# A depthwise convolution whose images share their padding and whose kernel rows sit in a deeper ring

## The chip, the cores and the metric

The kernel runs on one core of a Trainium2 chip. The metric is the device time of one execution in microseconds (us); the time given is the median of several executions. A separate, profiled execution gives the records that the tables show.

## The reference

The program is four layers on a batch of 8 images of 384 channels and 32 x 32 points. Layers 0 and 1 are state-space blocks, the second with an MLP. The change touches only what follows them:

```
# layer 2: depthwise 13x13, plus six smaller and dilated depthwise kernels, each with its own scale and shift
out = bn(dwconv(x, w_lk, 1)) + sum(bn(dwconv(x, w, r)) for w, r in branches)
# layer 3: a pointwise product, then depthwise 13x13 and a per-channel factor, then gelu
x_pw = bn(einsum('bchw,oc->bohw', x, pw_w)) + x
out = gelu(bn(dwconv(x_pw, dwk_w)) + bn(x_pw * dw1_w))
```

All is in float32. The kernel folds the seven branches of layer 2 into one 13 x 13 kernel per channel, and the per-channel factor of layer 3 into the centre of its kernel.

## The kernel before

Three stages follow the state-space layers: a depthwise convolution (tensor x3 to x4), the pointwise product (x4 to x5), and a second depthwise convolution (x5 to the output). The last MLP of the layers writes x3 in three thirds of 128 channels (`mlp_out`, L714, and `mlp_store`, L721); its two products are the matmuls of L695 (first) and L708 (second). That part has an order written out by hand. The three stages after it are issued in the order that the framework finds from the program's order and its waits.

x3 and x5 hold, for each channel, image row and image, 32 points between two gaps of six zeros, so WIDE = 44 columns. The eight images of one row lie behind each other: 352 numbers.

A depthwise convolution (`Depthwise.run`) handles four channels at a time, a group; 96 groups make the 384 channels. Its work per group:

- Two image transfers on GpSimd's queue (L958) put the 32 rows of four channels into a tile `xp`, two channels on partitions 0 to 31 and two on 64 to 95, the second shifted by two numbers.
- Four kernel transfers (L962), one for each shift of one column, put windows of the kernel table into a tile `wt`, 64 KB each. Two go over SyncE's queue, one over ScalarE's and one over GpSimd's.
- Four copies on VectorE (L975 twice, L976, L977) fill the other partitions of `xp` with the same rows shifted by one or two numbers. They cover two channels of n - 1 or n - 2 numbers, n = 8 x WIDE.
- Sixteen matmuls on TensorE (L982): for each of four column offsets (4j) and four channels, 128 partitions by 32 columns of weights against 8 images x 32 points.
- One activation on ScalarE (L987) adds the bias and takes the result out of PSUM, and a store on ScalarE's queue (L988) writes it.

`xp` and `wt` are rings of eight tiles. Before group 0, six groups are loaded; in group g the transfers of group g + 6 are issued (AHEAD = 6). A tile is free for its next transfer when the matmuls of the group eight earlier, group g - 2, have read it. All 16 tiles are cleared on GpSimd when the object is made (L949), and the three output tiles of the pointwise stage after them (L1005). The memory of these tiles partly lies over tiles of the layers before; a first write waits until those have been used.

The pointwise stage (`Pointwise.run`) takes 16 blocks of 512 points: a load on SyncE's queue (L1011), nine matmuls for each of them (L1016), activation, an addition on VectorE (L1021) into a tile with gaps, and one store on ScalarE's queue.

A queue's issues run in the order in which they stand in its engine's program. The built program also gives every transfer one of eight semaphores, eight for those of SyncE and ScalarE together and eight for GpSimd's, in turn; an issue waits for the earlier transfer on its semaphore.

Of the kernel before, what the change touches and what calls it, by code (L numbers as in the profile page):

```python
# [9 lines left out]
F32 = mybir.dt.float32  # L10
# [6 lines left out]
P = 128  # L17
B = 8
# [9 lines left out]
HW = 32  # L28
# [4 lines left out]
HK = 64  # L33
KP = 4
PAD = KS // 2
WIDE = HW + 2 * PAD
NG = C // 4
EPS = 1e-5
PAST = 16100
# [27 lines left out]
class Plan:  # L67
# [3 lines left out]
    def __init__(self):  # L71
        self.slots = {}
# [151 lines left out]
def layers(tc, k, a, vec, x0, x1, x2, x3, lasting, got):  # L224
# [16 lines left out]
    with ExitStack() as st:  # L241
# [39 lines left out]
        nc.vector.memset(carry[:, KD], 0.0)  # L281
        rows_out = wp.tile([P, T // HW, WIDE], F32, name="rows_out")
        nc.gpsimd.memset(rows_out, 0.0)
# [648 lines left out]
class Depthwise:  # L932
# [4 lines left out]


    NB, AHEAD = 8, 6

    def __init__(self, tc, st):
        nc = self.nc = tc.nc
        self.keep = st.enter_context(tc.tile_pool(name="d_keep", bufs=1, reuse_waits="tile"))
        self.work = st.enter_context(tc.tile_pool(name="d_work", bufs=4, reuse_waits="tile"))
        self.psum = st.enter_context(tc.tile_pool(name="d_ps", bufs=4, space=PSUM, reuse_waits="tile"))
        self.wts = [self.keep.tile([P, 4, HW, KP], F32, name=f"wt{i}") for i in range(self.NB)]
        self.xps = [self.keep.tile([P, 4, B * WIDE], F32, name=f"xp{i}") for i in range(self.NB)]
        for t in self.wts + self.xps:
            nc.gpsimd.memset(t, 0.0)  # L949

    def load(self, g, src, table):
        nc, n = self.nc, B * WIDE
        wt, xp = self.wts[g % self.NB], self.xps[g % self.NB]
        for h in range(2):
            rows = bass.AP(
                src.tensor, src.offset + (g * P + 2 * HW * h) * n + 2 * h, [[n, HW], [HW * n, 2], [1, n - 2 * h]]
            )
            nc.gpsimd.dma_start(xp[2 * HW * h : 2 * HW * h + HW, 2 * h : 2 * h + 2, 0 : n - 2 * h], rows)  # L958
        for s, queue in enumerate((nc.sync, nc.scalar, nc.sync, nc.gpsimd)):
            at = table.offset + (16 * g + s) * HK * KP  # L960
            windows = bass.AP(table.tensor, at, [[KP, HW], [4 * HK * KP, 4], [1, HW * KP]])
            queue.dma_start(wt[HW * s : HW * (s + 1)].rearrange("p q r j -> p q (r j)"), windows)  # L962

    def run(self, src, table, bias, func, store):
        nc = self.nc
        n = B * WIDE
        for g in range(self.AHEAD):
            self.load(g, src, table)
        for g in range(NG):
            wt, xp = self.wts[g % self.NB], self.xps[g % self.NB]  # L970
            if g + self.AHEAD < NG:
                self.load(g + self.AHEAD, src, table)
            for h in range(2):
                low, q = 2 * HW * h, slice(2 * h, 2 * h + 2)
                nc.vector.tensor_copy(xp[low + HW : low + 2 * HW, q, 0 : n - 1], xp[low : low + HW, q, 1:n])  # L975
            nc.vector.tensor_copy(xp[2 * HW :, 0:2, 0 : n - 2], xp[: 2 * HW, 0:2, 2:n])  # L976
            nc.vector.tensor_copy(xp[: 2 * HW, 2:4, 2:n], xp[2 * HW :, 2:4, 0 : n - 2])  # L977
            ps = self.psum.tile([P, T], F32, tag="ps", name="ps")
            x = xp.rearrange("p q (b c) -> p q b c", c=WIDE)
            for j in range(KP):  # L980
                for q in range(4):
                    nc.tensor.matmul(  # L982
                        ps[HW * q : HW * (q + 1), : B * HW], wt[:, q, :, j], x[:, q, :, 4 * j : 4 * j + HW],
                        start=j == 0, stop=j == KP - 1,
                    )
            o = self.work.tile([P, B, HW], F32, tag="o", name="o")
            nc.scalar.activation(o, ps[:, : B * HW], func, bias=bias[:, g : g + 1])  # L987
            nc.scalar.dma_start(store(g), o)  # L988
# [42 lines left out]
@with_exitstack  # L1031
def network(ctx: ExitStack, tc: tile.TileContext, a: dict, out: bass.AP):
    nc = tc.nc
    const = ctx.enter_context(tc.tile_pool(name="const", bufs=1))
    dram = ctx.enter_context(tc.tile_pool(name="dram", bufs=1, space=DRAM))

    k = {}
    k["avg"] = const.tile([P, P], F32, name="avg")
    nc.vector.memset(k["avg"], 1.0 / C)
    k["eps"] = const.tile([P, 1], F32, name="eps")  # L1040
    nc.vector.memset(k["eps"], EPS)
    k["one"] = const.tile([P, 1], F32, name="one")
    nc.vector.memset(k["one"], 1.0)
    k["minus"] = const.tile([P, 1], F32, name="minus")
    nc.vector.memset(k["minus"], -1.0)
    k["fold"] = const.tile([P, 32], F32, name="fold")
    k["gate"] = const.tile([P, KC * B], F32, name="gate")
    k["gate_b"] = const.tile([P, KC * B], F32, name="gate_b")
    vecs = const.tile([P, NVEC], F32, name="vecs")
    nc.sync.dma_start(vecs, a["vecs"])  # L1050

    def vec(name):
        at, width = VEC[name]
        return vecs[:, at : at + width]

    x_in = a["x"].rearrange("b c h w -> b c (h w)")
    x0 = [x_in[b] for b in range(B)]
    x1 = [dram.tile([C, L], F32, name=f"x1_{b}") for b in range(B)]
    x2 = [dram.tile([C, L], F32, name=f"x2_{b}") for b in range(B)]
    x3 = dram.tile([C, HW, B, WIDE], F32, name="x3")  # L1060
    x4 = dram.tile([C, HW * B * HW], F32, name="x4")
    x5 = dram.tile([C, HW * B * WIDE], F32, name="x5")

    k["one_at_R"] = vec("one_at_R")
    got = {"b2": const.tile([P, NG], F32, name="b2"), "b3": const.tile([P, NG], F32, name="b3")}
    got["pw"] = const.tile([P, 2 * KC], F32, name="pw_norm")
    layers(tc, k, a, vec, x0, x1, x2, x3, dram, got)

    with ExitStack() as st:

        past = st.enter_context(tc.tile_pool(name="past", bufs=1, reuse_waits="tile"))
        past.tile([P, PAST], F32, name="past")
        past_ps = st.enter_context(tc.tile_pool(name="past_ps", bufs=1, space=PSUM, reuse_waits="tile"))
        past_ps.tile([P, 4 * T], F32, name="past_ps")
        conv = Depthwise(tc, st)
        point = Pointwise(tc, st, conv.psum, a["pw"])
        x4_rows = x4.rearrange("c (r n) -> (c r) n", r=HW)
        conv.run(
            x3, got["k2"], got["b2"], AF.Identity,
            lambda g: x4_rows[g * P : (g + 1) * P].rearrange("p (b w) -> p b w", w=HW),  # L1080
        )
        point.run(x4, x5, got["pw"][:, 0:KC], got["pw"][:, KC:])
        out_rows = out.rearrange("b c h w -> (c h) b w")
        conv.run(x5, got["k3"], got["b3"], AF.Gelu, lambda g: out_rows[g * P : (g + 1) * P])
# [113 lines left out]
```

## Time and profile before

| | us |
|---|---|
| median of 3 executions | 6946.22 |
| range | 6943.45 to 6947.82 |
| the profiled execution's own time | 6954.78 |
| its span | 6952.9 |
| first copy of the first convolution | 6373.28 |
| first pointwise matmul | 6599.89 |
| first copy of the second convolution | 6734.08 |

| over the whole span | busy us | share |
|---|---|---|
| TensorE, matmuls | 5904.4 | 85% |
| TensorE, weight loads | 2097.6 | 30% |
| VectorE | 5851.6 | 84% |
| ScalarE | 4475.0 | 64% |
| GpSimd | 5429.7 | 78% |

How to read what follows: PE is TensorE (PEld its weight loads), DVE VectorE, ACT ScalarE, POOL GpSimd, SP SyncE. L982 is line 982 of the kernel before. In a timeline, a row gives the start and the duration in us, the engine, the line, the operation, the tiles, how many instructions are merged, and in brackets the idle time before and what ended it. In a list of waits a row gives who waited for whom, the total in us, how often, and the longest. In a table of stretches a row gives the stretch, its length and each engine's busy time. The DMA share is the mean busy share of 16 DMA engines; transfers overlap in it, so it can exceed 1. Transfers issued by GpSimd are instructions with a duration of their own in its timeline, one per transfer.

The three last stages take 580 us of the span of 6952.9. The busy shares of the page are nearly all of the layers before them, so the stages are to be read by themselves.

### The profile page before, as it was taken

What the parts mean: (1) busy time and instruction counts of PE and PEld (TensorE: products, weight loads), DVE (VectorE), ACT (ScalarE), POOL (GpSimd) and SP (SyncE); (2) the same over time, 40 slices, a digit from 0 to 9 for tenths busy, and PEclk for the clock granted to TensorE, in tenths of its full rate; (3) what the DMA queues carried; (4) which work ended last, traced back from release to release, by engine and by line L of the source; (5) the groups of instructions that cost most, each with busy time, mean ns of one, the idle gap of its engine ahead of it and who ended that gap; (6) DMA issues with size and microseconds to landing.
All of it is one profiled execution on the core that took longest, in us unless ns stands there. A gap on an engine that the chain in (4) does not pass through costs nothing. (4 is left out here: it accounts for less than half of the span.)

```text
span 6952.9 us, 78464 instructions
## 1 busy us (share of the span) xinstructions
PE 5904.4 (85%) x22562; PEld 2097.6 (30%) x22562; DVE 5851.6 (84%) x4975; ACT 4475.0 (64%) x7478; POOL 5429.7 (78%) x3146
## 2 busy tenths in 40 slices
PE   6777788888888888888888888888889889877898
PEld 2222222222322232222222232223223223324645
DVE  2899998999889888888889988988888998863849
ACT  4776666767676767767676767676677667742222
POOL 2888888888788878888888878887877888754626
PEclk7888898999999999999999999999999889999999
DMA  4665555666666566666666665656666666645979
GB/s 123 166 176 155 154 160 149 167 168 173 171 165 181 157 169 167 161 168 167 167 165 172 167 174 161 176 155 174 165 157 168 160 171 172 161 108 131 264 224 242
DMA packets 960565, 1169.60 MB, mean 168 GB/s; under 512 B 314057, under 2 KB 552713, under 8 KB 960137
## 3 DMA queue, kind: packets, MB, share of 16 engines
q1 hardware_dynamic: 787848, 1062.39, 57.5%
q10 hardware_dynamic: 147712, 55.08, 3.1%
q0 software_dynamic: 24576, 47.12, 2.3%
q8 instruction: 184, 3.01, 0.2%
q14 instruction: 245, 2.00, 0.1%
HBM read 909.39 MB, written 204.21 MB: 160 GB/s over the span
## 5 line engine op out<-in xcount | busy, mean ns | idle before, releaser
L532 POOL TENSOR_TENSOR dbu<-B,ru 128x1024 f32<-128x1024 f32 x1536 | 3584.9, 2357 | 136.9 <-DMA B<-bc 56.8
L525 ACT ACTIVATE h<-rd,A 128x512 f32<-128x512 f32 x3072 | 2117.5, 691 | 861.8 <-DVE hc L561 524.8
L553 DVE TENSOR_TENSOR_SCAN h<-h,state,dbu 128x512 f32<-128x512 f32 x1152 | 1482.4, 1287 | 221.1 <-ACT h L525 79.6
L561 DVE TENSOR_TENSOR hc<-h,C 128x1024 f32<-128x1024 f32 x1152 | 1410.8, 1225 | 129.2 <-PE acc L583 14.5
L556 DVE TENSOR_TENSOR_SCAN h<-h,dbu 128x1024 f32<-128x1024 f32 x576 | 1318.1, 2288 | 239.0 <-ACT h L525 182.4
L572 POOL TENSOR_TENSOR hc<-dbu,C 128x1024 f32<-128x1024 f32 x384 | 903.5, 2353 | 736.7 <-DVE dbu L556 337.1
L583 PE MATMUL acc<-hc,fold 128*32 128x512 f32 x6144 | 1174.6, 663 | 340.7 <-DVE hc L561 257.9
L415 PE MATMUL mm<-xt,wi 128*128 128x512 f32 x2232 | 1123.3, 642 | 43.6 <-ACT delta L491 18.9
L695 PE MATMUL f<-mx,wi 128*128 128x512 f32 x1152 | 610.5, 638 | 139.9 <-ACT fh L699 111.0
L708 PE MATMUL f<-fh,wo 128*128 128x512 f32 x1152 | 587.0, 628 | 82.0 <-DMA wo<-in_fc_dram 66.8
L415 PEld LDWEIGHTS mm<-xt,wi 128*128 128x128 f32 x2232 | 424.7, 202 | 745.4 <-issue 447.8
L604 PE MATMUL mm<-u,wo 128*128 128x512 f32 x1152 | 579.4, 643 | 38.5 <-DMA wo<-in_l_out_dram 31.4
L583 PEld LDWEIGHTS acc<-hc,fold 128*32 128x32 f32 x6144 | 165.9, 112 | 1163.7 <-DVE hc L561 548.5
L553 DVE TENSOR_TENSOR_SCAN dbu<-h,state,dbu 128x512 f32<-128x512 f32 x384 | 470.4, 1267 | 14.0 <-ACT h L525 8.6
L556 DVE TENSOR_TENSOR_SCAN dbu<-h,dbu 128x1024 f32<-128x1024 f32 x192 | 437.9, 2281 | 39.8 <-ACT h L525 29.3
L439 PE MATMUL mm<-xp,taps 128*64 128x512 f32 x1536 | 407.0, 653 | 33.8 <-DMA xp<-xp 12.4
L982 PE MATMUL ps<-xp,wt 128*32 128x256 f32 x6144 | 376.1, 387 | 66.0 <-DVE xp L977 30.3
L958 POOL DMA_DIRECT2D xp<-x x384 | 215.4, 565 | 276.8 <-DMA x<-q_out 139.8
L305 ACT ACT_TABLE_LOAD x289 | 370.8, 1283 | 5.9 <-PEq L1186 0.7
L695 PEld LDWEIGHTS f<-mx,wi 128*128 128x128 f32 x1152 | 209.3, 196 | 499.4 <-issue 248.5
L580 PE MATMUL acc<-u,skip 128*128 128x512 f32 x384 | 226.8, 675 | 153.7 <-DVE u L588 153.5
L425 ACT ACTIVATE xp<-mm,b_in 64x512 f32<-64x512 f32 x384 | 261.5, 681 | 140.8 <-PE mm L415 138.3
(152 smaller groups left out, 5876.2 us busy)
## 6 DMA issues: line engine op xcount, KB each, us to landing
ru<-uu SPq DMA_DIRECT2D x1536, 128.0 KB
rd<-dd SPq DMA_DIRECT2D x1536, 128.0 KB
wi<-w_in SPq DMA_DIRECT2D x372, 192.0 KB
xp<-xp SPq DMA_DIRECT2D x384, 128.5 KB
dd<-delta SPq DMA_DIRECT2D x192, 256.0 KB
uu<-delta SPq DMA_DIRECT2D x192, 256.0 KB
wo<-in_l_out_dram SPq DMA_DIRECT2D x96, 384.0 KB
wi<-fc_w SPq DMA_DIRECT2D x192, 192.0 KB
```

What stands on the lines that cost most here:

```text
L415: nc.tensor.matmul(s.ps[m], w[:, c], s.xt[:, c], start=c == 0, stop=c == KC - 1)
L439: nc.tensor.matmul(s.ps[d][64 * h : 64 * h + 64], taps[:, h, j], xp[h][:, 2 * j : 2 * j + T], start=j == 0, stop=j == 1,)
L525: nc.scalar.activation(y[:, q], s.dr[d][1][h][:, q], AF.Exp, scale=s.layer.A[:, at : at + 1])
L532: nc.gpsimd.tensor_tensor(dbu, s.B[g].unsqueeze(1).to_broadcast([P, 2, T]), s.ur[d][1][h], ALU.mult)
L553: nc.vector.tensor_tensor_scan(to[:, q], y[:, q], dbu[:, q], first, ALU.mult, ALU.add)
L556: nc.vector.tensor_tensor_scan(flat_to, flat_y, flat_b, first, ALU.mult, ALU.add)
L561: nc.vector.tensor_tensor(hc, to, s.C[g].unsqueeze(1).to_broadcast([P, 2, T]), ALU.mult)
L572: nc.gpsimd.tensor_tensor(hc, y, s.C[g].unsqueeze(1).to_broadcast([P, 2, T]), ALU.mult)
L583: nc.tensor.matmul(s.acc[d][32 * r : 32 * r + 32], k["fold"], tiles[r // 2][:, r % 2], start=False, stop=n == PER - 2)
L604: nc.tensor.matmul(s.ps[m], w[:, d], s.us[d], start=d == 0, stop=d == KD - 1)
L695: nc.tensor.matmul(s.ps[m], s.w["in", m][:, c], s.xt[:, c], start=c == 0, stop=c == KC - 1)
L708: nc.tensor.matmul(s.down, s.w["out", 2 * m + f // KD][:, f % KD], s.hs[f], start=f == 0, stop=f == KF - 1)
```

## The change

It does three things.

- The gap between two images of a row is shared: six zeros instead of twelve, WIDE = 38. A row of eight images has 304 numbers. The last image needs a gap behind it, so an `xp` tile has 12 numbers more than a row's, which stay zero. The matmuls take their 8 x 32 points from a slice that begins at 4j. The stored tensors x3 and x5 and the tiles that are written to them are narrower in the same way.
- The kernel rows have a ring of 24 tiles of their own (`NK`), of 2 KB a partition each, that is no longer cleared first. In group g the kernel transfers of group g + 22 are issued (`EARLY`), over the same queues as before; the images stay 6 ahead in a ring of 8.
- The kernel transfers of the first 22 groups are issued by a new function `early`, all four of each group on GpSimd's queue: for the first convolution ahead of its image transfers, for the second after the first convolution and ahead of the pointwise stage.

```diff
-WIDE = HW + 2 * PAD
+WIDE = HW + PAD
...
     NB, AHEAD = 8, 6
+    NK, EARLY = 24, 22
...
-        self.wts = [self.keep.tile([P, 4, HW, KP], F32, name=f"wt{i}") for i in range(self.NB)]
-        self.xps = [self.keep.tile([P, 4, B * WIDE], F32, name=f"xp{i}") for i in range(self.NB)]
-        for t in self.wts + self.xps:
+        self.wts = [self.keep.tile([P, 4, HW, KP], F32, name=f"wt{i}") for i in range(self.NK)]
+        self.xps = [self.keep.tile([P, 4, B * WIDE + 2 * PAD], F32, name=f"xp{i}") for i in range(self.NB)]
+        for t in self.xps:
             nc.gpsimd.memset(t, 0.0)
 
-    def load(self, g, src, table):
+    def kernels(self, g, table, queues):
+        wt = self.wts[g % self.NK]
+        for s, queue in enumerate(queues):
+            at = table.offset + (16 * g + s) * HK * KP
+            windows = bass.AP(table.tensor, at, [[KP, HW], [4 * HK * KP, 4], [1, HW * KP]])
+            queue.dma_start(wt[HW * s : HW * (s + 1)].rearrange("p q r j -> p q (r j)"), windows)
+
+    def early(self, table):
+
+        for g in range(self.EARLY):
+            self.kernels(g, table, [self.nc.gpsimd] * 4)
+
+    def images(self, g, src):
         nc, n = self.nc, B * WIDE
-        wt, xp = self.wts[g % self.NB], self.xps[g % self.NB]
+        xp = self.xps[g % self.NB]
...
-        for s, queue in enumerate((nc.sync, nc.scalar, nc.sync, nc.gpsimd)):
-            at = table.offset + (16 * g + s) * HK * KP
-            windows = bass.AP(table.tensor, at, [[KP, HW], [4 * HK * KP, 4], [1, HW * KP]])
-            queue.dma_start(wt[HW * s : HW * (s + 1)].rearrange("p q r j -> p q (r j)"), windows)
...
         for g in range(self.AHEAD):
-            self.load(g, src, table)
+            self.images(g, src)
         for g in range(NG):
-            wt, xp = self.wts[g % self.NB], self.xps[g % self.NB]
+            wt, xp = self.wts[g % self.NK], self.xps[g % self.NB]
             if g + self.AHEAD < NG:
-                self.load(g + self.AHEAD, src, table)
+                self.images(g + self.AHEAD, src)
+            if g + self.EARLY < NG:
+                self.kernels(g + self.EARLY, table, (nc.sync, nc.scalar, nc.sync, nc.gpsimd))
...
-            x = xp.rearrange("p q (b c) -> p q b c", c=WIDE)
             for j in range(KP):
+                x = xp[:, :, 4 * j : 4 * j + n].rearrange("p q (b c) -> p q b c", c=WIDE)
                 for q in range(4):
                     nc.tensor.matmul(
-                        ps[HW * q : HW * (q + 1), : B * HW], wt[:, q, :, j], x[:, q, :, 4 * j : 4 * j + HW],
+                        ps[HW * q : HW * (q + 1), : B * HW], wt[:, q, :, j], x[:, q, :, 0:HW],
...
+        conv.early(got["k2"])
         conv.run(
             x3, got["k2"], got["b2"], AF.Identity,
...
+        conv.early(got["k3"])
         point.run(x4, x5, got["pw"][:, 0:KC], got["pw"][:, KC:])
```

## The prediction

> **What bounds the kernel now.** I read the busy time by stretch first, then the timelines of VectorE, GpSimd and TensorE at the borders of the stages, then the waits and the chain. Stretches: first convolution from 6373 us, pointwise from 6599, second convolution from 6734 (columns: length, then busy us and instructions of PE, PEld, DVE, ACT, POOL, then clock, DMA share, GB/s).
>
> ```profile
> 6373.00:6590.00 217.00, 184.51 (x3060) 144.31 (x3064) 200.43 (x385) 44.84 (x95) 159.52 (x280) 0.97 0.93 259
> 6599.00:6727.00 128.00, 125.53 (x288) 55.28 (x288) 33.24 (x48) 37.30 (x48) 0.00 (x0) 0.98 0.66 219
> 6734.00:6947.00 213.00, 188.59 (x3048) 111.22 (x3048) 200.34 (x384) 44.80 (x95) 152.48 (x276) 0.99 1.06 249
> ```
>
> VectorE (DVE) works 200 us in each convolution, 384 copies. Its timeline shows that this is all it can do:
>
> ```profile
> 6387.61 0.52 DVE L975 COPY xp<-xp 32x702 f32<-32x702 f32 x1
> 6388.17 0.52 DVE L977 COPY xp<-xp 64x700 f32<-64x700 f32 x1
> ...
> 6390.38 0.52 DVE L977 COPY xp<-xp 64x700 f32<-64x700 f32 x1
> 6394.02 0.52 DVE L975 COPY xp<-xp 32x702 f32<-32x702 f32 x1 [3.12 <-PE ps L982]
> ```
>
> A copy starts every 0.551 us (0.522 at work, 0.030 between), so a group of four takes 2.206 and 96 groups 211.8. From 6373.28 to 6589.09 (215.8 us) the only wait is the 3.12 above; from 6734.08 to 6946.91 (212.8 us) there is none. VectorE is the bound of both. The runners-up are close. TensorE needs 1.96 us for a lone group, some 1.8 back to back (96 records, three groups, in 5.51). The stores on ScalarE's queue:
>
> ```profile
> ACT o L987 <- DMA out_dram<-o: 92.3, 57, 2.6
> PEld ps L982 <- DVE xp L977: 66.0, 93, 0.9
> ```
> ```profile
> 6429.88 3.99 DMA x<-o
> ...
> 6433.95 4.42 DMA x<-o
> ...
> 6438.45 5.23 DMA x<-o
> ```
>
> As built, a DMA issue on the SP or ACT queue waits for the eighth before it; a group issues four there, so a store waits for the store two groups back. In the first convolution TensorE starts 12 us late for want of kernel rows and catches up from 6403 to 6523 with 1,862 matmul records in 120 us, 32 a group: 2.06 us, 2.05 allowing for the 0.6% of records that the table shows missing of 3072. The chain of that time is stores of about 4.1 us each, two groups apart. So the store loop can do some 2.05, at DMA share 0.97.
>
> What sets the start of the first convolution is seen in GpSimd's (POOL's) timeline and TensorE's:
>
> ```profile
> 6302.64 5.46 POOL L1005 MEMSET q_out<- 128x2112 f32 x3
> 6360.43 1.27 POOL L958 DMA_DIRECT2D xp<-x  x2 [52.34 <-issue]
> 6361.70 0.56 POOL L962 DMA_DIRECT2D wt<-k_rows  x1
> 6362.24 1.07 POOL L958 DMA_DIRECT2D xp<-x  x2
> ```
> ```profile
> 6335.45 2.84 PE L695 MATMUL f<-mx,wi 128*128 128x512 f32 x6 [0.78 <-ACT fh L699]
> ```
>
> POOL stands idle from 6308 to 6360 (until x3's first third is stored) and issues images 13 us before VectorE, busy with its last residual add until 6373.25, takes them. That is all the slack an insertion in POOL's queue has there.
>
> [...] the trace has 2.31 from the first issue at 6731.77 to the copy at 6734.08. [...] an issue takes 0.54 us while VectorE rests, 0.57 beside it.
>
> **The change, part by part.**
> Narrower rows (44 to 38 columns, 352 to 304 an image row). Copies shrink from 702 and 700 to 606 and 604 elements: [...] with the same 0.030 between, 2.006 us a group. Saved 0.200 x 96 = 19.2 us in each convolution. The matmuls keep their 256 columns; their rows start at 8-byte instead of 16-byte steps, which I cost at nothing (bounds: 0 and, if a group rose from 1.96 to 2.1, +9 per convolution). The pointwise output falls from 1056 to 912 KB: 0.4 us off the last store (4.00 us in the chain), which opens the second convolution. x3's stores are hidden behind matmuls.
>
> Kernel rows 22 ahead. In steady state the queues carry the same 256 KB of kernels a group, the four issues each still after TensorE's group g-2; only the last 22 groups have none. The images fall from 175 to 152 KB, so a group moves 536 instead of 559 KB (-4.2%).
>
> The early loads, first convolution. 22 groups x 4 = 88 issues, all on POOL, ahead of the images. When can they start? The memsets of the old eight kernel tiles (3.8 us) go. But the tiles now reach further into memory of the layers: as built, the memset of the third q_out waits for the matmuls of the last first-MLP slice, which end at 6335.45 + 2.84 = 6338.3. With its 1.6 us (1824 elements at the row's 1858 ns for 2112) the first early issue comes at 6339.9. 88 x 0.54 = 47.5 (48 to 50 at 0.55 to 0.57), so POOL is free for images at 6387.4 to 6390; I take 6388.2. Plus the 2.3 us of the second convolution's start: first copy at 6390.5 instead of 6373.28, 17.2 us late. In return the kernels are there, and the 3.1 us wait goes. First convolution: copies end at 6390.5 + 192.6 + 0.5 = 6583.6, against 6589.1: -5.5.
>
> The early loads, second convolution. 88 issues, queued on POOL after image group 95, each tile after its last matmul: from about 6569 to 6618, 64 KB every 0.55 us, 119 GB/s beside the pointwise (219). Its matmuls take all 125.5 us and had one wait for a load, the first of 8.8 us; the sum of 338 GB/s is below the 390 that the trace shows in bursts. POOL's next work, images at 6732, waits anyway. Six groups of kernel loads that stood before the first pointwise input on the SP queue shrink to two, so I put the delay of that input at +0.5 (bounds -0.5 and +2).
>
> Second convolution: -19.2 -0.4. Its stores have 128-byte packets and the share is 1.06; no stretch shows how fast its store loop can go, only 2.206. Scaled from 2.05 by DMA share and bytes, 2.05 x 1.06/0.97 x 0.958 = 2.15; with slack, 2.006, for TensorE never waits for ACT there. For the 74 groups with kernels I take 2.05, nearer to the lower: +3.3 (bounds 0 and +10.7). In the first, 2.05 x 0.958 = 1.96 is below VectorE's 2.006: nothing.
>
> Sum: -5.5 + 0.5 - 19.2 - 0.4 + 3.3 = -21.3 us. The profiled execution took 6954.78 (span 6952.9), the median is 6946.22, 8.6 less; the difference lies in no stage, so I take the saving whole: 6946.2 - 21.3 = 6925.
>
> **The rivals.**
> (1) The start isn't late, because early issues fit in POOL's idle 52 us: for it, the idle time is longer than 47.5; against it, 30 us of it lie before the memset is released. 6925 - 17.2 = 6908.
> (2) The store loop takes the bound over in part, 2.06 to 2.15 in both convolutions. For it: stores already hold ACT for 92 us of 213, about 1 us behind TensorE. Against: ACT never holds TensorE in the second one. Without the 3.3 the sum is -24.6; with 148 groups x 0.054 to 0.144 us more, 6930 to 6943, middle 6936.
> (3) It ends slower: the store loop doesn't quicken at all. Place: the store's wait for the store two groups back. At 2.206 for the 148 groups with kernels, -24.6 + 148 x 0.2 = +5: 6951. It decides from 2.17, where 148 x (p - 2.006) is 24.6; from 2.27 it is over 0.2%.
> (4) The change doesn't do what it says (copies as long as before): 6946.2 - 24.6 + 38.4 = 6960; [...]
>
> **How the numbers follow.** Forecast 0.64 (6916 to 6932), (1) 0.05, (2) 0.18, (3) 0.10, (4) 0.03. 0.2% is 13.9 us, about what a measurement can tell: faster below 6932.3. The forecast nearly whole, (1) and a little of (2): faster 0.72. The rest of (2) and most of (3): same 0.23. Slower 0.05. Range: leave out (1), the upper half of (3) and (4): 6912 to 6946.
>
> **What would show it.** Right: copies of 0.472 us, 0.502 apart; POOL's first early issue near 6340 and first image near 6388; first copy near 6390; copies end near 6584; no 3.1 us wait; second convolution some 194 to 197 us. Wrong: images issued near 6360; VectorE waiting for images while ACT waits for stores (rivals 2, 3); the first pointwise input over 2 us later after the last copy than 10.8.

## The result and the profile after

| | before | after |
|---|---|---|
| median | 6946.22 us | 6968.72 us |
| range of 7 executions each | 6941.35 to 6951.60 | 6962.32 to 6977.39 |
| ratio, 95% interval | | 1.0033 [1.0021, 1.0044] |
| profiled execution (span) | 6954.78 (6952.9) | 6964.66 (6962.7) |

The change made the kernel 0.33% slower, 22.5 us between the medians. The forecast was 21.3 us faster.

Here are the stretches of after (the same columns as before: length, busy us and instructions of PE, PEld, DVE, ACT, POOL, then clock, DMA share, GB/s), from the first copy of each convolution and from the first pointwise matmul:

```profile
6406.00:6608.00 202.00, 189.54 (x3068) 111.52 (x3070) 187.52 (x384) 45.03 (x95) 159.22 (x285) 0.98 0.86 237
6618.00:6746.00 128.00, 126.42 (x288) 55.58 (x288) 32.53 (x47) 37.20 (x48) 27.09 (x51) 0.98 0.71 230
6753.00:6957.00 204.00, 184.00 (x3042) 146.64 (x3046) 185.57 (x384) 44.55 (x94) 147.09 (x261) 0.98 1.02 228
```

VectorE is busy 187.5 and 185.6 us instead of 200. Its timeline shows a late first copy, and copies that are not all of one length:

```profile
6406.65 0.47 DVE L986 COPY xp<-xp 32x606 f32<-32x606 f32 x1 [29.86 <-DMA xp<-x]
6407.16 0.49 DVE L987 COPY xp<-xp 64x604 f32<-64x604 f32 x1
...
6411.88 0.52 DVE L986 COPY xp<-xp 32x606 f32<-32x606 f32 x1
...
6417.80 0.47 DVE L987 COPY xp<-xp 64x604 f32<-64x604 f32 x1
6418.30 0.47 DVE L986 COPY xp<-xp 32x606 f32<-32x606 f32 x1
```

In the first convolution the list of waits of after has TensorE waiting for VectorE, so the copies are the bound there, and ScalarE waiting less for stores than in before, whose line comes last:

```profile
PEld ps L993 <- DVE xp L988: 52.7, 92, 0.8
ACT o L998 <- DMA x<-o: 47.4, 31, 4.0
```
```profile
ACT o L987 <- DMA x<-o: 79.4, 53, 3.8
```

VectorE has nothing to copy for 29.86 us after its last residual addition. TensorE's and GpSimd's timelines of after say why:

```profile
6338.15 2.84 PE L695 MATMUL f<-mx,wi 128*128 128x512 f32 x6 [0.78 <-ACT fh L699]
```

```profile
6341.05 1.62 POOL L1016 MEMSET q_out<- 128x1824 f32 x1 [35.00 <-PE f L695]
6342.62 10.49 POOL L957 DMA_DIRECT2D wt<-k_rows  x19
...
6363.18 5.95 POOL L957 DMA_DIRECT2D wt<-k_rows  x11 [4.26 <-DMA wt<-k_rows]
...
6374.07 7.03 POOL L957 DMA_DIRECT2D wt<-k_rows  x13 [4.05 <-DMA wt<-k_rows]
6383.34 1.09 POOL L957 DMA_DIRECT2D wt<-k_rows  x2 [2.24 <-DMA wt<-k_rows]
...
6387.98 16.22 POOL L957 DMA_DIRECT2D wt<-k_rows  x30 [0.50 <-DMA wt<-k_rows]
6404.18 7.37 POOL L971 DMA_DIRECT2D xp<-x  x14
```

The 88 early issues run from 6342.62 to 6404.18. In the brackets the queue waits for earlier early loads to land; the ten waits of that timeline come to 13.7 us. The images follow only then. The chain of waits of that time has three of these loads, each with the time until it let the queue go on:

```profile
6353.99 8.64 DMA wt<-k_rows
...
6365.34 8.45 DMA wt<-k_rows
...
6379.47 8.22 DMA wt<-k_rows
```

The last MLP itself is hardly longer beside them: from its last first matmul to the last residual addition it takes 35.8 us in after and 35.0 in before.

In the second convolution TensorE now waits for ScalarE, which the list of waits of before did not have in that stage, and the chain of waits of that time is stores again, two groups apart. Of the 9.9 us that VectorE waits for images, 6.7 lie before its first copy:

```profile
ACT o L998 <- DMA out_dram<-o: 60.2, 40, 3.3
PEld ps L993 <- ACT o L998: 34.4, 43, 2.0
DVE xp L986 <- DMA xp<-x: 9.9, 4, 6.7
```
```profile
6782.15 4.16 DMA out_dram<-o
...
6786.39 6.15 DMA out_dram<-o
...
6792.61 3.68 DMA out_dram<-o
```

Here is where the time of the last three stages lies, from the end of the last residual addition (us, from the timelines). "Between" is from the last copy of the first convolution to the first copy of the second, "end" from the last copy to the end of the span. Most of the experiments below are in the same table; their names are explained with them. Each ratio is taken to executions of before that ran beside that kernel on the same chip. The groups e1 to e4, e5 to e8, e9 to e12 with e16 and e17, e13 to e15, and e18 ran on five different chips, so ratios can be compared between groups and plain times cannot.

| kernel | start | copies 1 | between | copies 2 | end | sum | ratio to before, 95% interval |
|---|---|---|---|---|---|---|---|
| before | 0.0 | 215.8 | 145.0 | 212.8 | 6.0 | 579.7 | 1 |
| after | 29.9 | 200.0 | 146.8 | 202.8 | 6.5 | 585.9 | 1.0033 [1.0021, 1.0044] |
| e1 rows only | 0.0 | 201.5 | 152.3 | 202.4 | 12.4 | 568.6 | 1.0007 [0.9999, 1.0015] |
| e2 ring only | 17.8 | 212.6 | 144.3 | 213.0 | 5.7 | 593.4 | 1.0033 [1.0020, 1.0046] |
| e3 early first | 0.0 | 198.7 | 147.9 | 197.0 | 5.7 | 549.5 | 0.9982 [0.9974, 0.9991] |
| e5 before again | 0.0 | 215.9 | 150.4 | 212.8 | 6.0 | 585.1 | 0.9996 [0.9987, 1.0004] |
| e6 half early | 0.0 | 198.7 | 144.8 | 204.6 | 10.3 | 558.4 | 1.0004 [0.9996, 1.0013] |
| e7 SyncE kernels | 0.0 | 200.1 | 150.5 | 202.5 | 9.9 | 563.1 | 1.0011 [1.0004, 1.0018] |
| e8 wide, early first | 0.0 | 213.0 | 144.1 | 213.0 | 5.7 | 575.9 | 0.9996 [0.9987, 1.0004] |
| e12 before, shifted | 0.0 | 215.7 | 146.2 | 212.5 | 7.1 | 581.4 | 1.0014 [1.0008, 1.0021] |
| e13 after, padded | 30.1 | 200.2 | 147.3 | 203.7 | 8.1 | 589.3 | 1.0015 [1.0008, 1.0021] |
| e14 rows only, padded | 0.0 | 204.8 | 151.2 | 204.9 | 12.8 | 573.7 | 0.9999 [0.9991, 1.0007] |
| e16 even tiles, rows of 40 | 0.0 | 202.5 | 144.7 | 202.2 | 6.1 | 555.6 | 0.9930 [0.9917, 0.9942] |
| e17 even tiles, rows of 38 | 0.0 | 197.5 | 147.9 | 199.4 | 7.5 | 552.2 | 0.9950 [0.9937, 0.9964] |
| e18 after, rows of 40 | 17.4 | 202.7 | 145.6 | 203.9 | 8.4 | 578.0 | 0.9990 [0.9983, 0.9997] |

By this table after loses 6.2 us in the three stages, of 22.5 between the medians. Some 16 us are missing. The two traces by themselves do not show them: the last residual addition ends at 6376.79 us in after and at 6373.25 in before, only 3.5 apart. But the traced execution of before took 8.6 us more than its median, and that of after 4.1 less. If the stages are as long in the other executions, most of the missing time lies in the layers ahead of the change. That became the second question.

### The profile page after: what moved, and what is told of

It reads as the page before. It is cut to its first block, busy times and chain, and to the rows that moved or that the text cites. A ratio compares the mean times of both kernels' runs of the same rounds, so it can differ in the third digit from the quotient of the medians.

```text
span 6962.7 us, 78501 instructions
## 1 busy us (share of the span) xinstructions
PE 5895.9 (85%) x22562; PEld 2095.8 (30%) x22562; DVE 5826.3 (84%) x4975; ACT 4474.8 (64%) x7478; POOL 5495.7 (79%) x3270
## 5 line engine op out<-in xcount | busy, mean ns | idle before, releaser
L604 PE MATMUL mm<-u,wo 128*128 128x512 f32 x1152 | 576.2, 640 | 50.4 <-DMA wo<-in_l_out_dram 42.9
L553 DVE TENSOR_TENSOR_SCAN dbu<-h,state,dbu 128x512 f32<-128x512 f32 x384 | 470.4, 1267 | 10.8 <-ACT h L525 6.1
```

What stands on the lines that cost most here:

```text
L553: nc.vector.tensor_tensor_scan(to[:, q], y[:, q], dbu[:, q], first, ALU.mult, ALU.add)
L604: nc.tensor.matmul(s.ps[m], w[:, d], s.us[d], start=d == 0, stop=d == KD - 1)
```

## The experiments

The theory after the first look was: the late start (29.9 us) eats what narrower rows bring, and copies stretch beside GpSimd's issues. The rivals were that narrower rows bring nothing, or that the deep ring costs something wherever it is loaded.

### One part of the change alone: e1, e2, e3, e8

e1 is before with narrower rows (`WIDE = HW + PAD`, the longer `xp` tile, the matmuls' slice) and the old ring. e2 is after with the wide rows, the `xp` tile and the slice of before, and a ring of 20, which makes room for the wide tiles. e3 is after with one line moved, e8 is e3 with wide rows:

```diff
 e2, e8:
-WIDE = HW + PAD
+WIDE = HW + 2 * PAD
-    NK, EARLY = 24, 22
+    NK, EARLY = 20, 18
 e3, e8:
         conv = Depthwise(tc, st)
+        conv.early(got["k2"])
         point = Pointwise(tc, st, conv.psum, a["pw"])
...
-        conv.early(got["k2"])
```

> The kernel before with the narrower rows alone (kernel ring of 8, loads 6 ahead, as before). Theory: the loss of the change lies in the early kernel loads that stand ahead of the first images on GpSimd's queue, and the rows are a gain that is smaller than forecast, because a copy that runs beside a GpSimd issue takes the pace of the issues (0.52 to 0.53 us instead of 0.502). So the first copy comes near 6373 to 6376 us, a group takes 2.08 us instead of 2.206, each convolution is 10 to 12 us shorter, and the time is 6946 - 22 = 6924 (6920 to 6930). Rival, that the narrow rows themselves cost (their 8-byte steps, their transfers, the stretched copies): no gain, 6946 or more.

> The change with the wide rows of before, and a ring of 20 with 18 groups early (24 and wide rows do not fit in memory together); 72 early issues on GpSimd's queue. Theory: the first copy is late by the issues and their waits for landing, 72/88 of the 62 us seen after the change, so some 51 us from 6340: 6393 instead of 6373, near 20 us late; the copies run back to back at 2.206 us a group, since the issues are then faster than the copies; the time is 6946 + 17 to 25, 6963 to 6971. Rival, that the early loads are harmless and the rows are the loss: 6943 to 6950.

> The change, with the early kernel loads of the first convolution issued before the pointwise stage's tiles are cleared, so that they do not wait for the last first-MLP matmuls: GpSimd starts them near 6303 us and is through in 50 to 62 us, 6353 to 6365, when x3's first third is ready. Theory: the first copy comes at 6376 to 6380, right after VectorE's last residual add, the 30 us are gone, and the time is 6969 - 30 = 6939, still short of the rows alone only by what the second convolution loses to its stores. Rival, that the early loads hurt by their traffic beside the MLP's weights: the MLP's matmuls wait for weights in turn, and the time stays above 6955.

> The ring of the changed kernel with the old wide rows (20 tiles, 18 groups early, as the wide rows leave no room for 24) and the early loads moved ahead of the other clears: the ring without its late start and without narrower rows. Theory: copies every 0.552 us, 212.5 in each convolution, no start wait; stages about 577, that is 3 us below before, ratio 0.9995 to 1.0005. Rival (the ring loads bring a gain or a loss of their own): under 0.998 or over 1.002.

e3 settles the start. The early loads now stand ahead of the memsets of `q_out`, which wait for the last first-MLP matmul, and are done before the images can come. GpSimd's timeline of e3:

```profile
6291.12 22.38 POOL L957 DMA_DIRECT2D wt<-k_rows  x41
...
6341.35 4.75 POOL L1016 MEMSET q_out<- 128x1824 f32 x3
6350.13 7.51 POOL L971 DMA_DIRECT2D xp<-x  x14 [4.02 <-DMA x<-rows_out]
```

The images wait for x3 and for nothing else. The first copy follows the last residual addition at once (start 0.0), and the kernel is faster than both, 0.9982. e2 has the ring with the late start and without narrower rows. Its start is 17.8 us late and it is slower by 0.33%, as expected; with the early loads moved (e8) it is level with before. That e2's total agrees is in part luck: its three stages are only 11 us longer than before's (593.4 against 582.4, the mean of its two traces, e5 below), and the other 13 us of 24 are not explained.

e1 was a miss. Its copies do fall by 14 and 10 us, but the time did not. Two things take it back. In its three stages "end" is 6 us longer and "between" 2 to 7 us (against the two traces of before, with e5 below), so that 11 to 16 of 25 us are left. And those are not in the median either, which points to the layers again.

### What stretches the copies: e4, e7

e4 is e1 with every transfer of the loop on SyncE's and ScalarE's queues. e7 is e3 with only the kernel transfer of GpSimd moved to SyncE:

```diff
 e4:
-            nc.gpsimd.dma_start(xp[...], rows)
-        for s, queue in enumerate((nc.sync, nc.scalar, nc.sync, nc.gpsimd)):
+            nc.sync.dma_start(xp[...], rows)
+        for s, queue in enumerate((nc.sync, nc.scalar, nc.sync, nc.scalar)):
 e7:
-                self.kernels(g + self.EARLY, table, (nc.sync, nc.scalar, nc.sync, nc.gpsimd))
+                self.kernels(g + self.EARLY, table, (nc.sync, nc.scalar, nc.sync, nc.sync))
```

> The narrow rows alone, with no transfer of the convolutions issued by GpSimd: images on SyncE's queue, kernels on SyncE's and ScalarE's. Made for the length of the copies, not for the time: with seven transfers a group on eight semaphores the pace will be set by the transfers, 2.3 us a group or more, 6950 to 7000 us. Theory of the copies: all of them take 0.472 us, as none runs beside a GpSimd issue. Rival, that the copies were stretched by transfers writing the same tiles: they still take 0.49 us in the mean, with single ones of 0.51 to 0.53.

> The kernel with the early loads ahead, and in the loop GpSimd's kernel transfer of each group on SyncE's queue instead, so that GpSimd issues two transfers a group and not three. Theory (a copy on VectorE is stretched from 0.472 to 0.49 or more only beside a transfer issue of GpSimd): a third of the stretch goes, 2 us less in each convolution, first 196.7, second about 195; ratio 0.997. Rival (five transfers a group now share the eight semaphores of SyncE's and ScalarE's queues, so the store waits for one 1.6 groups back): groups of 2.1 to 2.3 us while kernels are loaded, 10 to 20 us more in each convolution, ratio 1.001 to 1.004.

e4 took 7152.57 us in its one execution, far more than expected: seven issues a group share the eight semaphores of the two queues, and VectorE waits 241.5 us for images. But it answers its question. The copies by line, with the least, the median and the longest in ns:

```profile
L975 DVE COPY xp<-xp x384: 465/468/471, 6373.0 to 7144.1; 32x606 f32<-32x606 f32 x192
L976 DVE COPY xp<-xp x192: 469/469/473, 6373.5 to 7143.6; 64x604 f32<-64x604 f32 x192
```

Without a transfer issue of GpSimd no copy takes over 473 ns. In after the longest takes 558 to 566. Sorting after's first convolution by GpSimd's records gives 256 copies that lie wholly beside issues, 0.492 us on average and one every 0.525, and 29 beside none, 0.469 and one every 0.502. In before the same sorting gives 0.522 and 0.519: on average the wide copies were hardly touched. The size varies from trace to trace: copies beside issues take 0.489 us in e3 and 0.480 in e9 (below), whose convolutions have the same code. A copy beside issues loses 0.02 us on average and never more than 0.10 in after, not the 0.54 that an issue takes.

The two timelines of after's first convolution show which copies lose it. Of the 256, 182 have an issue that starts later than 0.1 us after their own start, and take 0.501 us on average; 38 with an issue that starts in their first 0.1 us take 0.469, and 36 in which none starts 0.468, none of these 74 over 0.471. In before, 65 of 228 copies beside issues have a late one, and take 0.530 (0.605 at most); 137 with an early one and 26 with none take 0.519 and 0.518. So it is the place of an issue's start in the copy that goes with the loss, in both kernels, and narrow copies have it late more often. What an issue's start does to the copy is not shown; nor is why it falls late in narrow ones. The author's guess for the second is that narrow copies come faster than the issues (one every 0.502 us against 0.54) and wide ones do not (0.551).

In e7 the copies beside issues are fewer (149 copies, 0.477 us), as the theory has it, and it gains nothing by it: five transfers a group on the other two queues make ScalarE wait 113 us for kernel loads in each convolution. The ratio, 1.0011, is the rival's, though the rival's 10 to 20 us more in each convolution do not come: the copies span 1.4 and 5.5 us more than in e3.

### Half the early loads: e6

```diff
-    NK, EARLY = 24, 22
+    NK, EARLY = 13, 11
```

> The changed kernel with a ring of 13 and 11 groups early instead of 24 and 22. Theory (the start is late because the early issues stand ahead of the images on GpSimd's queue): 44 issues take 25 to 31 us instead of 61.6, images are issued some 27 to 33 us after the last first-MLP matmul, and the first copy comes 0 to 2 us after the last residual addition instead of 30; time about that of the kernel with the early loads moved ahead, ratio 0.997 to 0.999. Rival (the deep ring or its transfers cost, wherever they stand): 1.001 to 1.003.

With a ring of 13, in after's place, the start is not late (0.0), but not for the expected reason alone. The images were expected some 27 to 33 us after the last first-MLP matmul. Here the clearing of `q_out` does not wait for that matmul at all (presumably a smaller ring puts those tiles elsewhere in memory; not shown), and the early issues begin 33 us before its end (6347.31 us). GpSimd's and TensorE's timelines of e6:

```profile
6309.19 4.74 POOL L1016 MEMSET q_out<- 128x1824 f32 x3
6313.88 17.51 POOL L957 DMA_DIRECT2D wt<-k_rows  x32
```
```profile
6344.47 2.84 PE L695 MATMUL f<-mx,wi 128*128 128x512 f32 x6 [0.78 <-ACT fh L699]
```

So e6 does not tell what fewer early issues are worth by themselves; that the start hangs on GpSimd's queue rests on after's timeline and on e3. The time, 1.0004, lies between the two figures. The second convolution, from its first copy to the end, takes 214.9 us against 209.2 in after; 85 instead of 74 groups load kernels beside their stores, which fits.

### Are the layers slower? The control: e5

> The kernel before, unchanged, as a control, since narrower rows alone shortened the two convolutions of their trace by 14 and 10 us and yet the time did not fall. Theory (the last three stages of before are as long as in its first trace, and the layers before them wander by chance): ratio 1.000 +- 0.001, and from the end of the last MLP matmul to the end of the span 580 us again (first trace: 6372.5 to 6952.9). Rival (the first trace of before was untypical in its last stages): 565 to 570 us there, so that narrower rows with 569 gain nothing in the stages. Second rival (the comparison itself leans by the order of the runs): ratio above 1.001 for the same program.

The same program gives 0.9996 and 585.1 us in the three stages, 5 more than its first trace: neither the comparison nor that trace was odd. Then the median of each kernel less its stages tells what its layers take. Against before (its stages taken at 582.4, the mean of its two traces) the layers of after are some 19 us longer (22.5 - 3.5), those of e1 17.5, of e3 20, of e6 and e7 27 to 29; those of e2 and e8, with wide rows, 13 and 4. These differences carry the scatter of one trace, some 5 us, and that of the medians (after's interval is some 8 us to either side), so that e2's 13 cannot be told from e1's 17.5. But each of these kernels with narrower rows has 17 or more, and the change touches nothing there except for sizes: `rows_out`, the tile from which x3 is stored, is 384 bytes a partition smaller, and x3 is smaller in DRAM. In the built program the 7,542 work tiles of the layers lie behind `rows_out` and move by 384 bytes; x1, x2 and the scratch tensors that come after x3 move by 2.25 MiB.

### Which size does it: e9 to e12, e13, e14

```diff
 e9, e11, e13, e14:
-        rows_out = wp.tile([P, T // HW, WIDE], F32, name="rows_out")
+        rows_room = wp.tile([P, T // HW * 44], F32, name="rows_out")
+        rows_out = rows_room[:, : T // HW * WIDE].rearrange("p (r c) -> p r c", c=WIDE)
 e10, e11:
-    x3 = dram.tile([C, HW, B, WIDE], F32, name="x3")
+    x3_room = dram.tile([C * HW * B * 44], F32, name="x3")
+    x3 = x3_room[: C * HW * B * WIDE].rearrange("(c h b w) -> c h b w", h=HW, b=B, w=WIDE)
 e12 (on before):
         nc.gpsimd.memset(rows_out, 0.0)
+        room = wp.tile([P, 32], F32, name="room")
+        nc.gpsimd.memset(room, 0.0)
```

e9, e10 and e11 are made from e3, e13 from after, e14 from e1.

> The kernel with the early loads ahead, and rows_out allocated with its old 2816 bytes a partition, of which the first 2432 are used. Narrower rows had moved every work tile of the state-space layers by 384 bytes in on-chip memory, and x1, x2 and the scratch tensors allocated after x3 by 2.25 MiB in DRAM; here the on-chip addresses are those of before again. Set against their medians, the last three stages of the kernels with narrow rows leave 17 to 30 us more for the layers than those of the control. Theory A (the on-chip shift slows the layers): the layers lose 17 to 30 us, ratio 0.994 to 0.996. Theory B (the DRAM shift slows them): as the kernel with the early loads ahead, 0.998. Theory C (chance, or the narrower store itself): 0.998.

> The kernel with the early loads ahead, and x3 allocated with its old 17.3 MB in DRAM, of which the first 14.9 are used, so that the DRAM addresses are those of before and the on-chip ones stay shifted. Theory A (on-chip shift): 0.998. Theory B (DRAM shift): 0.994 to 0.996. Theory C: 0.998.

> Both paddings together, on the kernel with the early loads ahead: all addresses of the layers as before. Theories A and B: 0.994 to 0.996, that is the 30 us which its last three stages are shorter than those of the control. Theory C: 0.998.

> The kernel before with one unused tile of 128 bytes a partition behind rows_out, so that every work tile of the layers moves by 128 bytes, which is the narrow rows' shift of 384 modulo 512; nothing else is changed. Theory A (the address modulo 512 matters): the layers take 17 to 30 us more, ratio 1.0025 to 1.004. Theories B and C: 1.000.

> The changed kernel with rows_out allocated with its old 2816 bytes, and nothing else changed. Theory A (the on-chip shift of the layers' work tiles costs the layers 10 to 16 us): ratio 1.0010 to 1.0018, that is only the 6 us which the last three stages are longer, with some us for the early loads beside the last MLP. Rival (the loss is all in the last three stages, or in the DRAM addresses): 1.0033 again.

> Narrower rows alone on the kernel before, with rows_out allocated with its old 2816 bytes. Theory A: the gain of 11 to 16 us in the last three stages, which was hidden by the layers' loss, shows: ratio 0.998 to 0.9985. Rival (the padding brings its gain only beside the ring): 1.0007 again.

| | ratio, 95% interval | |
|---|---|---|
| e3 | 0.9982 [0.9974, 0.9991] | both shifted |
| e10 | 0.9984 [0.9977, 0.9991] | DRAM restored |
| e9 | 0.9966 [0.9953, 0.9980] | on-chip tiles restored |
| e11 | 0.9954 [0.9938, 0.9970] | both restored |
| e12 | 1.0014 [1.0008, 1.0021] | before, on-chip tiles shifted |
| e13 | 1.0015 [1.0008, 1.0021] | after (1.0033), on-chip tiles restored |
| e14 | 0.9999 [0.9991, 1.0007] | e1 (1.0007), on-chip tiles restored |

Restoring the DRAM addresses does nothing. Restoring the on-chip places gives after 0.18% back, 12.5 us, with intervals that only touch; from e10 to e11, which ran beside each other, it gives 0.30%, with intervals apart. Shifting them in before costs 0.14%, some 10 us (under the 17 to 30 expected). That the places cost time is shown; the size is known only as 0.1 to 0.3%. e14 missed its figure: with the places restored narrower rows alone still bring nothing, although their stages are some 9 us shorter.

The records of the DMA packets say what is slower. VectorE's and ScalarE's instructions in the layers last as long in all kernels (scans 1617 or 1618 ns on average, activations 654). Packets do not. Mean ns of a packet in the first 6200 us, by its size:

| kernels | 512 B | 2048 B | 2056 B | x3's stores |
|---|---|---|---|---|
| before, e2, e5, e8 (176-byte rows) | 35.7 to 36.9 | 115.1 to 117.9 | 142.0 to 143.2 | 20.0 to 21.2 |
| e12 (before, shifted) | 37.3 | 118.2 | 147.9 | 19.9 |
| after, e1, e3, e6, e7, e10 (152-byte rows, shifted) | 37.0 to 37.6 | 118.0 to 120.8 | 148.3 to 149.0 | 24.7 to 28.6 |
| e9, e11, e13, e14 (152-byte rows, restored) | 35.8 to 36.4 | 116.8 to 118.9 | 142.3 to 143.7 | 25.7 to 28.9 |

The built programs give the places of the tiles. In before most work tiles begin 96 bytes behind a multiple of 256, and shifted ones 224 behind; the tiles of nearly all 512-byte and 2048-byte rows of the layers are among them. The 2056-byte rows go to tiles 224, 0, 32 and 64 bytes behind such a multiple in before, and 96 to 192 shifted. From the first line of the table to the third the packets rise in all three sizes (by 2%, 3% and 4%). In e12 nothing else is changed, and they rise there too: the 2048-byte ones to 118.2 ns, by 1%, the 2056-byte ones to 147.9. So the shift alone makes packets longer; by what it does so is not shown.

The last column was not expected: x3's stored rows are shorter by 24 bytes and take 5 to 8 ns longer than wide ones on the same chip.

### Tiles at even places, and rows of 40: e15 to e18

e15 is e11 with 680 numbers for `rows_out`, by which 5,914 of the work tiles begin at multiples of 512; e17 is e15 once more, beside e16, which is e15 with rows of 40. e18 is after with rows of 40, whose tiles move by 256 bytes, so that their places modulo 256 are those of before. Their ring of 22 makes room for the wider tiles.

```diff
 e15, e16, e17:
-        rows_room = wp.tile([P, T // HW * 44], F32, name="rows_out")
+        rows_room = wp.tile([P, 680], F32, name="rows_out")
 e16, e18:
-WIDE = HW + PAD
+WIDE = HW + 8
-    NK, EARLY = 24, 22
+    NK, EARLY = 22, 20
```

> The kernel with the early loads ahead and x3 padded, with rows_out allocated at 2720 bytes instead of 2816 or 2432: 5914 of the layers' 7542 work tiles then begin at a multiple of 512 bytes, instead of 96 behind one (as before) or 224 behind one (narrow rows). If transfers to on-chip memory take longer the further from a multiple of 512 their tile begins, the layers gain once more: ratio 0.993 to 0.995, and the 2056-byte packets of the layers take under 142 ns. If only the old place was good by chance: 0.996 to 0.999, packets at 143 to 149 ns.

> The kernel with the work tiles at multiples of 512 bytes, with rows of 40 numbers an image instead of 38 (a gap of eight zeros), and a ring of 22 with 20 groups early, since 24 no longer fit. Theory (a stored row of 152 bytes that begins at no multiple of 32 costs more than one of 160 that does): the x3 packets take 18 to 21 ns instead of 25 to 29, the layers get 3 to 10 us back; the copies grow from 0.472 to 0.489 us, which costs 3 to 6 us in each convolution; together within 0.1% of the same kernel with 38. Rival (the packets are slow for another reason, as the writes of more and shorter segments): 25 ns or more again, and 0.1 to 0.2% slower than with 38.

> The kernel with the work tiles at multiples of 512 bytes and rows of 38 again, beside the one with rows of 40 on the same chip. Both theories: ratio 0.9935 to 0.996 to the kernel before, x3 packets of 25 to 29 ns.

> The changed kernel with rows of 40 numbers an image instead of 38, and a ring of 22 with 20 groups early (24 no longer fit); the early loads stay where the change put them. Theory (the layers lost 10 us by shifted work tiles and 5 to 20 by stored rows of 152 bytes): the layers are as before or faster, 2056-byte packets 142 to 144 ns, x3 packets 18 to 21 ns; the last three stages some 5 us longer than in the changed kernel for longer copies, less 5 for eight early transfers fewer; ratio 0.999 to 1.001 instead of 1.0033. Rival (the loss belongs to the late start and the loop alone): 1.003 again.

| | ratio, 95% interval | 512 B | 2048 B | 2056 B | x3's stores |
|---|---|---|---|---|---|
| e15 | 0.9948 [0.9934, 0.9961] | 33.3 | 115.1 | 147.0 | 29.2 |
| e17 | 0.9950 [0.9937, 0.9964] | 33.0 | 114.0 | 146.5 | 27.3 |
| e16 | 0.9930 [0.9917, 0.9942] | 33.1 | 112.2 | 146.2 | 19.1 |
| e18 | 0.9990 [0.9983, 0.9997] | 36.7 | 117.4 | 142.2 | 18.9 |

In e15 the 512-byte rows of the layers, whose tiles now begin at a multiple of 512, take 33.3 ns, some 3 less than in before, while the 2056-byte ones, whose tiles come to lie 128 to 224 behind a multiple of 256, take 147.0, nearly as long as in the shifted kernels (148.3 to 149.0). The expectation of under 142 ns for these was wrong; it had not asked where those tiles would lie.

e16 is the surprise. Against e17 on the same chip the stores of x3 fall from 27.3 to 19.1 ns, and the median from 6906.10 to 6886.56 us, although the three stages are 3.4 us longer. The expectation had been no difference. So rows of 152 bytes cost about 20 us in that kernel, and more than that in its layers (the rings differ too, by two tiles, and with them the early loads). e16 is the fastest of all, 50.4 us under before.

e18 is the same edit in the changed kernel, late start and all, and turns 1.0033 into 0.9990, some 30 us; its tiles lie 256 bytes from their places in before, and its packets of 512, 2048 and 2056 bytes take as long as there (36.7, 117.4 and 142.2 ns). Its stages are 7.9 us shorter than after's (578.0, with a start of 17.4 us), so some 22 us of it come from the layers. That is the places and the row length together. Against e13, which has only the places restored, e18 is 0.25% quicker, 17 us; 11.3 of these lie in the stages (589.3 and 578.0), which leaves some 6 us in the layers for the row length, within the scatter of a trace. The queue of SyncE and ScalarE from 1000 to 6200 us (packets, MB, share of the 16 engines' time), of before, after and e18:

```profile
q1 hardware_dynamic: 605232, 856.45, 62.1%
```
```profile
q1 hardware_dynamic: 605464, 854.77, 64.4%
```
```profile
q1 hardware_dynamic: 605209, 855.02, 61.4%
```

After moves fewer bytes in that time than before and its packets take more time for them; rows of 40 take less than before.

## Why the prediction was wrong

The direction was wrong: 21.3 us faster was forecast, 22.5 slower was measured. In the three stages three terms were too small: the early issues (12.6 us), the copies beside issues (6.9) and the store loop (5.9). The layers ahead of the stages were put at nothing, which was the largest single miss (16 us).

**What bounds the kernel**: right for both convolutions, but for 4.8 us in the second. The copies of after are 0.47 us where nothing is beside them (forecast 0.472, an estimate for which before had no copy of that width), 0.50 apart (0.502).

**"First copy at 6390.5 instead of 6373.28, 17.2 us late"**: the mechanism was right, down to the memset of `q_out` (forecast to release the first early issue at 6339.9; it came at 6342.62, with its matmuls 2.7 us later than before). The size failed in the term "88 x 0.54 = 47.5": the issues themselves take 61.6 - 13.7 = 47.9 us, but the term left out that an issue waits for the earlier load on its semaphore to land. The text before the prediction had named the eight semaphores, and the prediction used them for the stores and not here. Start 29.9 us late: 12.6 more than forecast. The 3.1 us wait for kernels is gone, as forecast.

**"Narrower rows ... 0.502 apart, 2.006 us a group"**: the copies span 200.0 us in the first convolution, against 192.6 + 0.5: 6.9 more. The failing step is the one from "an issue takes 0.54 us while VectorE rests, 0.57 beside it" to no loss at all: these are lengths of issues, and neither is of a copy beside them. e4, with no copy over 0.473 us, shows that the stretch belongs to GpSimd's issues; its size varies (e9, with the same convolution, spans 196.5).

**"For the 74 groups with kernels I take 2.05"**: the second convolution's copies span 202.8 us instead of 212.8 - 19.2 + 3.3 = 196.9, 5.9 more, with 4.8 us of waits in the copies' timeline. The pace of the store loop that the 2.05 was scaled from was itself too short: the table of stretches of before has 1,795 matmul records from 6403 to 6523 us, 2.14 us a group, not 1,862 and 2.06. The store loop that rivals (2) and (3) named did take part of it: TensorE waits 34.4 us for ScalarE, and the chain is stores. How much it takes varies with the trace: e3, with the same code there, spans 197.0 without a wait.

**Small terms**: the pointwise input came 12.1 us after the last copy instead of 10.8 (+1.3, forecast +0.5); its matmuls took 126.4 us (+0.9, forecast 0); the last `q_out` store 3.73 us (-0.3, forecast -0.4); the end 0.5 more.

The sum of the stages: -21.3 + 12.6 + 6.9 + 5.9 + 0.8 + 0.9 + 0.1 + 0.5 = +6.4; the traces show +6.2.

**"x3's stores are hidden behind matmuls"** and the saving taken whole for the median: this step failed too, and it made the difference between +6 us, which is within 0.2%, and +22.5. The working looked only at the last three stages: it put x3's stores at nothing and had no term for the places of other tiles. That `rows_out` sits ahead of the layers' work tiles, and that x3 is stored by the layers in packets of one image row each, was in the code (98,304 packets, 86,016 of them in the first 6200 us). The difference between the medians and the stages is 22.5 - 6.2 = 16 us, with the scatter given above. e13 shows 12.5 us of it to be the places of the tiles. The rest, some 4 us, is in the range of what the stored rows cost by e18 against e13 (some 6 us), while e16 against e17 has 20 for them. How much of after's loss is theirs stays open.

**The rivals.** (1) would have been right with one line moved: e3 has start 0.0. (4) is out. (3) named 6951 for a store loop that does not quicken at all; in the second convolution that is nearly what e1 and e14 do, whose ring of eight loads kernels to the end: from the first copy of the second convolution to the end 214.9 and 217.7 us, against 218.8 in before. The waits of e14 there:

```profile
ACT o L988 <- DMA out_dram<-o: 86.1, 55, 3.5
PEld ps L983 <- ACT o L988: 44.1, 54, 3.6
```

So narrower rows gain little there without the deep ring, whose last groups store without kernel loads beside them: after takes 209.2 there, e3 202.8. None of the rivals looked at the layers, and so slower had a chance of only 0.05.

## What to carry to other kernels

A change of a tile's or a tensor's size is also a change to every transfer of it and to the place of every tile behind it: before forecasting a stage, list all transfers whose rows change in length or in their start on chip (2056-byte packets took 147.9 ns here with a shift by 128 bytes, e12, and 142.2 with one by 256, e18, against 142.0 to 143.2 without), and the lengths of rows stored to DRAM (27.3 ns a packet at 152 bytes, 19.1 at 160, e17 and e16), wherever in the program they are. Loads that are to be early must stand in their queue ahead of the first wait for late data; moving one line was worth some 35 us here (1.0033 against 0.9982). If stages sum to another difference than the medians, run the old kernel again as a control, and look for the rest outside the stages.

## What the runs showed of the hardware

- A store of rows of 152 bytes, of which three in four begin at no multiple of 32 bytes, takes longer a packet (24.7 to 29.2 ns) than one of 176 (19.9 to 21.2) or of 160 at multiples of 32 (18.9 and 19.1). Rows of 176 bytes begin at no multiple of 32 either for every second image and take the 19.9 to 21.2 ns, so that alone is not the reason. 160 and 176 are multiples of 16, and 152 is not; no run here separates the length, the start in DRAM and the start on chip.
- Where a tile begins on chip shows in the packets of transfers to and from it, by 1 to 4% (e12: 118.2 ns for 2048 bytes, 147.9 for 2056, against 115.1 to 117.9 and 142.0 to 143.2), and 128 bytes of shift cost the whole kernel 0.14% (e12).
- A 0.47 us copy on VectorE takes 0.48 to 0.49 on average beside GpSimd's transfer issues (e9, e3, after) and 0.566 at most in after; without such issues none of e4's 768 takes over 0.473. One of 0.52 us hardly changes on average (before: 0.522 beside issues, 0.519 beside none). The loss is in the copies in which an issue starts later than 0.1 us after the copy's own start (after: 0.501 us, against 0.469 and 0.468 for the others; before: 0.530, against 0.519 and 0.518).
- GpSimd's queue runs at 0.54 us an issue only as long as its loads land in time: after's 88 early issues took 47.9 us of work and 13.7 of waits for loads, and beside the end of the MLP three of these loads took 8.2 to 8.6 us, by its chain of waits.
